# Early convolutions, gate sums and substitution steps of a delta-net and FFN kernel, placed elsewhere

## The chip, the core and the metric

The kernel runs on one core of one Trainium2 chip. The metric is the device time of one execution in microseconds. The core's engines each work through a queue of their own, in the order in which the program issues to them: PE multiplies matrices (PEld is its weight load), DVE, ACT and POOL work on tensors element by element, and SP issues the DMAs. An engine waits where an operand isn't ready or where the place for its result is still being read.

## What is computed

The reference, cut to the parts that the change touches, is a gated delta rule over 4 sequences of 1024 positions with 256 features, followed by a small FFN; each of the two is layer-normed and added to its input:

```python
mixed = einsum('bsh,ch->bsc', x, W_qkv)               # 16 q, 16 k, 32 v heads of 128
conv  = sum(xp[:, i:i+S, :] * conv_w[:, i] for i in range(4))
q, k, v = split(silu(conv))                           # q and k are then normed
beta  = sigmoid(x W_b);  g = -exp(A_log) * softplus(x W_a + dt_bias)
gc    = cumsum(g) within chunks of 64
A     = -(k_beta k^T * exp(gc_i - gc_j)) below the diagonal
Tm    = (I - A)^-1                                    # substitution
u, kcd = Tm v_beta, Tm (k_beta * exp(gc))
# scan over the chunks, with a state St of 128 x 128 for each head and sequence
v_new = u - kcd St
out_i = (q * exp(gc)) St + (q k^T * decay) v_new
St    = St * exp(g_last) + (k * exp(g_last - gc))^T v_new
out   = (rms_norm(out_i) * norm_w * silu(x W_z)) W_out
```

## The kernel before

**Before the main loop** (lines 194 to 281). The rows are read in four blocks of eight tiles, layer-normed and transposed into `xnT`, and the 64 gate columns of every position are summed into `ba` (L225). Then the gates are worked out on tiles of 128 x 1024 (L229 to L257). The cumulative sums follow for eight groups of four heads, one group at a time (L259 to L281): four products with triangular or constant matrices, exponentials on ACT into a table `dk`, a transpose for the rows `prow`, and three stores to DRAM, `rows_d` twice and `dk_d` once. The table `dk` has two buffers.

**The main loop** works on 32 blocks ("supers"), which are 8 groups of heads times 4 stretches of the sequence. Each has 8 units, and a unit is one turn of the loop: s counts from 0 to 255, with 21 early turns ahead of it (s = -21 to -1). A turn works at several stages of the pipeline at once. What it issues to PE, DVE, ACT and POOL is in an order written out by hand: eight strings in `SLOTS`, one for each turn of a round (`iq`, 0 to 7; I call it turn 0 to turn 7; for s >= 0, unit 0 falls on turn 5). SP's queue isn't in this order; it is placed by the framework. The letters are:

- A: one tile of v, and B: one tile of q or k, in the generator `channel`. PE makes the product `pp` in a pair of PSUM banks, ACT writes the first tap of the convolution into `cv` (L437), DVE adds three taps (L440), ACT applies the silu (L444). In the early turns before s = -4 there is only B.
- N0, N1, N2, O3, J, O4: the scan of a unit, in `step`. N0 transposes v (`pv`) and scales it into `x0`. N1 multiplies by the state (`pkqs`, L684), and DVE completes `x0` (L695) while ACT writes `qs` (L696). N2 makes `px` (L704), `xs`, `yg` (L712) and `kt`, and POOL decays the state (L721). In the next turn O3 makes `po` and `core` (L728), J the squares of it on ACT (L733), and O4 `pu` (L741), in a pair of banks, with the state's addition on DVE right behind it (L748).
- Z, T, U: the output projection of an older unit. Z makes `pz` (L143) and its silu; POOL multiplies `zs` twice (L784, L786); T transposes it; U makes `pout` (L797), and DVE adds it into `ac` (L802).
- s and n: scores and norms of a half super. POOL works on `dc` (L530, L531, L537), PE makes `kkq`, DVE `lT` and `aT` (L556), and `n` ends in four small operations on DVE (L488 to L502).
- v with a number: so many steps of the substitution, in `invert`. A step is two operations on DVE, L580 and L581, on (j+1)(31-j) elements for j from 0 to 30, all of it in SBUF. The first call only sets up the tiles.
- b: builds the rest of the inverse from it (`lb`'s copy on ACT, L593; `m1`, `m2` on PE). r and q: small operations of `rms` and the roots.

Two rules order what a letter issues. `go` takes a generator's next part, counts one place on, and then takes up whatever is due; a part that ends with `yield n` is due n places later. A `v` counts no place. `pp` (of A and of B) and `pu` share two pairs of PSUM banks in turn: A, `pu`, B, A, and so on.

A look-up table of the FFN's weights is expanded on POOL in 224 pieces, each a compare (L301) and, but for the first of 16, an addition (L305). One piece is issued behind O4 in every turn, from s = -21 on. From turn 240 the FFN's weights are fetched.

Of the kernel before, what the change touches and what calls it, by code (L numbers as in the profile page):

```python
# [9 lines left out]
F32 = mybir.dt.float32  # L10
I32 = mybir.dt.int32
AF = mybir.ActivationFunctionType
ALU = mybir.AluOpType
# [46 lines left out]
def bc(ap, shape):  # L60
    return ap.to_broadcast(shape)
# [3 lines left out]
def delta_net_ffn_kernel(  # L65
# [128 lines left out]
    with tc.tile_pool(name="pre", bufs=2) as pre, tc.tile_pool(name="gates", bufs=1) as gp:  # L194
# [6 lines left out]
        ba = gp.tile([P, NTILE, 2 * NV], F32, name="ba")  # L201
# [6 lines left out]
        for s in range(NSB):  # L208
# [16 lines left out]
            A.copy(ba[:, s * SB : (s + 1) * SB, :], pg.rearrange("p (t n) -> p t n", n=64))  # L225
        full = [P, NTILE, NV]
        gl = gp.tile(full, F32, name="gl")
        beta = gp.tile(full, F32, name="beta")
        A.activation(beta, ba[:, :, 0:NV], AF.Sigmoid)  # L229
        A.activation(nea, nea, AF.Exp)  # L230
        V.tensor_scalar_mul(nea, nea, -1.0)
        y = gp.tile(full, F32, name="y")
        u = gp.tile(full, F32, name="u")
        w = gp.tile(full, F32, name="w")
        d = gp.tile(full, F32, name="d")
        l = gp.tile(full, F32, name="l")
        V.tensor_tensor(y, ba[:, :, NV:], bc(dtr.unsqueeze(1), full), ALU.add)
# [17 lines left out]
        V.tensor_scalar_max(y, y, 0.0)  # L255
        V.tensor_add(y, y, l)
        V.tensor_tensor(gl, y, bc(nea.unsqueeze(1), full), ALU.mult)  # L257
        nth = NTILE * HG
        for g in range(NG):  # L259
            hs = slice(g * HG, (g + 1) * HG)  # L260
            dk = pre.tile([P, DK], F32, tag="dk", name="dk")
            ps = bank("pgate")
            for i, lhs in enumerate((triu, slow)):
                T_.matmul(ps[:, i * nth : (i + 1) * nth], lhsT=lhs, rhs=gl[:, :, hs], start=True, stop=True)
            A.activation(dk[:, 0 : 2 * nth], ps[:, 0 : 2 * nth], AF.Exp)
            V.tensor_copy(dk[:, 2 * nth : 3 * nth], ps[:, 0:nth])
            ps = bank("pgate")
            for ab in range(2):
                T_.matmul(
                    ps[:, ab * nth : (ab + 1) * nth], lhsT=sel[ab], rhs=gl[:, :, hs], start=True, stop=True  # L270
                )
            el = dk[:, 4 * nth : 6 * nth].rearrange("p (t a h) -> p a t h", a=2, h=HG)
            A.activation(el, ps[:, 0 : 2 * nth].rearrange("p (a t h) -> p a t h", a=2, h=HG), AF.Exp)
            V.tensor_copy(dk[:, 3 * nth : 4 * nth].rearrange("p (t h) -> p t h", h=HG), beta[:, :, hs])
            ps = bank("prow")
            T_.transpose(ps[:, :P], dk[:, 2 * nth : 3 * nth], ident)
            rows = pre.tile([P, P], F32, tag="rows", name="rows")
            A.copy(rows, ps[:, :P])
            for ab in range(2):
                nc.sync.dma_start(rows_d[g, ab], rows[:, ab * C : (ab + 1) * C])  # L280
            nc.sync.dma_start(dk_d[g], dk)  # L281
# [27 lines left out]
    with ExitStack() as main:  # L309
# [80 lines left out]
        def channel(k, blk, n, far):  # L390
# [47 lines left out]
            yield far  # L438
            for i in reversed(range(H)):
                V.scalar_tensor_tensor(cv, ps[:, :, i : i + BT], cw[:, ch, i : i + 1], cv, ALU.mult, ALU.add)  # L440
                if i == H - 1:
                    yield 1
# [215 lines left out]
        def step(k, u):  # L658
# [76 lines left out]
            if not last:  # L735
                pu = two_banks("pu")
                for m in range(MG):
                    two = slice(2 * m, 2 * m + 2)
                    for ab in range(2):
# [3 lines left out]
                        )  # L743
                state = S_.rearrange("p a h d -> p (a h d)")
# [98 lines left out]
        def work(kind, n, *args):  # L843
# [12 lines left out]

        LQ = 2 * SB + 5
        LV = SB // 2
        SLOTS = [
            "A v1 O3 s N0 v1 T n J O4 v1 N1 Z v1 B n N2 U n s",  # L860
            "A v1 O3 N0 v1 T J v1 O4 N1 r Z v1 B N2 q s U",
# [161 lines left out]
        with tc.manual_schedule(engines=COMPUTE):  # L1023
            for s in range(-LQ, len(units)):
# [13 lines left out]
                if nq < len(supers):  # L1038
                    gens["B"] = channel(supers[nq], iq // 4, iq % 4, 1)
# [119 lines left out]
```

## Time and profile before

| | us |
|---|---|
| median of 3 runs (4345.69 to 4350.42) | 4349.83 |
| the profiled execution | 4347.06 |
| its span, first to last instruction | 4345.3 |
| PE / DVE / ACT / POOL busy | 3992.3 / 3517.0 / 2646.9 / 2082.5 |
| before the first tile of the main loop (`pp` starts) | 110.45 |
| mean granted TensorE clock | 0.98 of full |

How it is read: times are in us unless marked ns. A line such as "L440 DVE ... cv<-pp,cw,cv 128x512 ... x1536 | 1148.9, 748 | 352.2 <-ACT cv L437 322.7" gives a line of the kernel, an engine, what is written from what, and the count; then the busy time, the mean length of one in ns, and the engine's idle time just before them with what ended most of it. A line of the timeline gives the start and the length, then the same names, and in brackets the idle time before. In the view by windows a line gives a stretch and its length, then busy time and count of PE, PEld, DVE, ACT and POOL, then the granted clock, the share of the DMA engines and GB/s. A wait for several semaphores is put down to the one that came last by the profile.

### The profile page before, as it was taken

What the parts mean: (1) busy time and instruction counts of PE and PEld (TensorE: products, weight loads), DVE (VectorE), ACT (ScalarE), POOL (GpSimd) and SP (SyncE); (2) the same over time, 40 slices, a digit from 0 to 9 for tenths busy, and PEclk for the clock granted to TensorE, in tenths of its full rate; (3) what the DMA queues carried; (4) which work ended last, traced back from release to release, by engine and by line L of the source; (5) the groups of instructions that cost most, each with busy time, mean ns of one, the idle gap of its engine ahead of it and who ended that gap; (6) DMA issues with size and microseconds to landing.
All of it is one profiled execution on the core that took longest, in us unless ns stands there. A gap on an engine that the chain in (4) does not pass through costs nothing.

```text
span 4345.3 us, 79442 instructions
## 1 busy us (share of the span) xinstructions
PE 3992.3 (92%) x26664; PEld 2858.5 (66%) x26664; DVE 3517.0 (81%) x6641; ACT 2646.9 (61%) x6573; POOL 2082.5 (48%) x1782
## 2 busy tenths in 40 slices
PE   3679999999999999999999999999999999999999
PEld 3456667677666666676766667676766776666454
DVE  4788888888888888888888988888888898886243
ACT  2456667666666666666666666666666666656211
POOL 2545564655555554655455554555554343434122
PEclk7899999999999999999999999999999999999999
DMA  3444444444444454444454444544445444443011
GB/s 88 124 107 113 111 112 124 121 130 119 126 130 118 107 133 125 134 117 119 125 135 128 109 114 128 133 118 114 132 128 128 115 120 121 130 108 96 26 39 29
DMA packets 1053124, 492.72 MB, mean 113 GB/s; under 512 B 730528, under 2 KB 951856, under 8 KB 1052720
## 3 DMA queue, kind: packets, MB, share of 16 engines
q1 hardware_dynamic: 1052720, 487.64, 42.5%
q8 instruction: 216, 3.54, 0.3%
q14 instruction: 188, 1.54, 0.1%
HBM read 267.66 MB, written 219.69 MB: 112 GB/s over the span
## 4 chain that ended last, share of the span: by engine, by line
PE 57%; DVE 25%; issue 7%; ACT 6%; POOL 3%; DMA 1%; SPq 1%; DVEq 0%; POOLq 0%; ACTq 0%
PE pp L423 13%; DVE cv L440 9%; PE pout L797 7%; PE pz L143 7%; PE pkqs L684 6%; DVE rank L580 4%; PE pgu L960 4%; PE px L704 4%; PE pu L741 3%; PE po L704 3%; DVE v L581 2%; PE kkq L546 2%; PE py L976 2%; DVE core L728 2%; PE pto L790 1%
## 5 line engine op out<-in xcount | busy, mean ns | idle before, releaser
L440 DVE SCALAR_TENSOR_TENSOR cv<-pp,cw,cv 128x512 f32<-128x512 f32 x1536 | 1148.9, 748 | 352.2 <-ACT cv L437 322.7
L784 POOL TENSOR_TENSOR zs<-zs,rr 128x512 f32<-128x512 f32 x256 | 267.0, 1043 | 1558.3 <-ACT zs L782 1549.3
L437 ACT ACTIVATE cv<-pp,cw 128x512 f32<-128x512 f32 x512 | 350.9, 685 | 486.0 <-PE pp L423 486.0
L581 DVE TENSOR_TENSOR v<-v,rank 128x31 f32<-128x31 f32 (+15 forms) x992 | 553.3, 558 | 34.1
L423 PE MATMUL pp<-xnT,wq 128*128 128x262 f32 x2048 | 531.0, 401 | 43.3 <-DVE cv L440 34.6
L423 PEld LDWEIGHTS pp<-xnT,wq 128*128 128x128 f32 x2048 | 371.7, 191 | 216.6 <-issue 58.7
L423 PE MATMUL pp<-xnT,wv 128*128 128x262 f32 x2048 | 503.0, 387 | 5.8 <-DVE cv L440 5.8
L797 PE MATMUL pout<-wo,oT 128*128 128x256 f32 x2048 | 504.9, 391 | 0.7 <-ACT oT L792 0.7
L143 PE MATMUL pz<-wzs,xnT 128*64 128x512 f32 x2048 | 487.1, 596 | 4.7 <-DVE ac L802 3.8
L580 DVE TENSOR_TENSOR rank<-v,lb 128x31 f32<-128x31 f32 (+15 forms) x992 | 467.2, 471 | 25.9 <-DMA lb<-ltd 20.1
L684 PE MATMUL pkqs<-S,qku 128*64 128x256 f32 x3840 | 478.1, 387 | 5.2 <-DVE core L728 3.5
L721 POOL TENSOR_TENSOR S<-S,dkm 128x1024 f32<-128x1024 f32 x224 | 436.7, 1949 | 26.5 <-PE pkqs L684 16.1
L704 PE MATMUL px<-x,ue 128*128 128x128 f32 x2048 | 292.9, 287 | 168.2 <-issue 108.1
L704 PEld LDWEIGHTS px<-x,ue 128*128 128x128 f32 x2048 | 264.1, 194 | 269.0 <-issue 151.1
L423 PEld LDWEIGHTS pp<-xnT,wv 128*128 128x128 f32 x2048 | 381.5, 190 | 73.8 <-issue 13.1
L797 PEld LDWEIGHTS pout<-wo,oT 128*128 128x128 f32 x2048 | 384.1, 198 | 49.4 <-issue 3.4
L684 PEld LDWEIGHTS pkqs<-S,qku 128*64 128x64 f32 x3840 | 248.7, 136 | 204.2 <-issue 49.2
L733 ACT ACTIVATE junk<-core 128x128 f32<-128x128 f32 x1024 | 318.5, 311 | 82.4 <-DVE core L728 53.9
L786 POOL TENSOR_TENSOR zs<-zs,core 128x512 f32<-128x512 f32 x256 | 328.6, 1284 | 20.0
L709 ACT ACTIVATE xs<-px 128x512 f32<-128x512 f32 x256 | 154.8, 605 | 236.2 <-PE px L704 236.2
L444 ACT ACTIVATE qk<-cv 128x512 f32<-128x512 f32 x256 | 161.2, 630 | 206.1 <-DVE cv L440 202.6
L741 PE MATMUL pu<-yg,kt 64*128 64x256 f32 x1920 | 272.2, 402 | 14.5 <-DVE cv L440 13.1
(187 smaller groups left out, 7198.4 us busy)
## 6 DMA issues: line engine op xcount, KB each, us to landing
qkd<-qk SPq DMA_DIRECT2D x256, 256.0 KB, 2.6
qku<-qkd SPq DMA_DIRECT2D x256, 256.0 KB, 2.9
dc<-rows_d SPq DMA_DIRECT2D x256, 128.0 KB, 3.4
ltd<-lT SPq DMA_DIRECT2D x128, 256.0 KB, 2.5
atd<-aT SPq DMA_DIRECT2D x128, 256.0 KB, 2.8
ae<-atd SPq DMA_DIRECT2D x512, 64.0 KB, 2.6
acc_d<-ac SPq DMA_DIRECT2D x256, 128.0 KB, 2.2
ac<-acc_d SPq DMA_DIRECT2D x224, 128.0 KB, 2.6
```

The costliest lines, as they stand in the source:

```text
L143: T_.matmul(ps[ab * C : (ab + 1) * C, :], lhsT=xnT[:, kc, 2 * p + ab, H + n * C : H + (n + 1) * C], rhs=rhs(kc), start=kc == 0, stop=kc == ...
L423: T_.matmul(ps[:, 2 * p : 2 * p + 2, : H + BT], lhsT=wt[:, kc, :], rhs=xnT[:, kc, 2 * p : 2 * p + 2, c0 : c0 + H + BT], start=kc == 0, sto ...
L437: A.activation(cv, ps[:, :, H : H + BT], AF.Copy, scale=cw[:, ch, H : H + 1])
L440: V.scalar_tensor_tensor(cv, ps[:, :, i : i + BT], cw[:, ch, i : i + 1], cv, ALU.mult, ALU.add)
L580: V.tensor_tensor(t, bc(v[:, 0 : j + 1, j : j + 1], sh), bc(lb[:, j : j + 1, j + 1 :], sh), ALU.mult)
L581: V.tensor_tensor(v[:, 0 : j + 1, j + 1 :], v[:, 0 : j + 1, j + 1 :], t, ALU.subtract)
L684: T_.matmul(as4(ps)[ab * C : (ab + 1) * C, two, :], lhsT=qk[:, m, j, ab, :], rhs=S_[:, ab, two, :], start=True, stop=True,)
L704: T_.matmul(as4(ps)[:, h, :], lhsT=w[:, h, :], rhs=src[:, h, :], start=True, stop=True)
L721: G_.tensor_tensor(flat, flat, bc(decay, [P, 2 * HG, P]), ALU.mult)
L741: T_.matmul(as4(pu[:, ab])[:, two, :], lhsT=kt[half, m, :], rhs=yg[half, two, :], start=True, stop=True)
L786: G_.tensor_tensor(zs, zs, k.cores.pop(u), ALU.mult)
L797: T_.matmul(pp[:, :HID], lhsT=oT[:, h, :], rhs=wo[:, h, :], start=h == 0, stop=h == HG - 1)
```

## The change

**Gates.** `ba` is laid out by groups of heads when it is copied out of PSUM. The maximum and the addition on `y` become one operation. The table `dk` holds all eight groups, `beta` is copied into it once, and the sums are made for four groups at a time: products with 512 columns instead of 128. The rows come from four products with the gates as the stationary operand, instead of a transpose. The number of stores is the same.

**Early tiles.** For B in the turns s = -20, -18, ..., -6, whose `far` is now 0, the three taps are scaled copies on ACT and additions on POOL, issued at once; for all other tiles the order is as before.

**The turns.** The state's addition behind `pu` is due two places later, which is behind N1. The steps of the substitution stand between A and Z in every turn, and none behind Z. The pieces of the look-up table are issued only from s = 0 on, and by turn: 1, 0, 1, 4, 1, 0, 1, 0.

```diff
@@ gates
-        ba = gp.tile([P, NTILE, 2 * NV], F32, name="ba")
+        ba = gp.tile([P, 2 * NG, NTILE, HG], F32, name="ba")
...
-        V.tensor_scalar_max(y, y, 0.0)
-        V.tensor_add(y, y, l)
-        V.tensor_tensor(gl, y, bc(nea.unsqueeze(1), full), ALU.mult)
...
+        V.scalar_tensor_tensor(l, y, 0.0, l, ALU.max, ALU.add)
+        V.tensor_tensor(by_group(l), by_group(l), heads(nea), ALU.mult)
+        dk = gp.tile([P, NG, DK], F32, name="dk")
+        V.tensor_copy(dk[:, :, 3 * GW : 4 * GW], beta.rearrange("p (g x) -> p g x", g=NG))
+        for gs in range(0, NG, 4):
+            cols = l[:, gs * GW : (gs + 4) * GW]
+            to = dk[:, gs : gs + 4]
             for i, lhs in enumerate((triu, slow)):
...
+                ps = bank("pgate")
+                T_.matmul(ps, lhsT=lhs, rhs=cols, start=True, stop=True)
+                ps = ps.rearrange("p (g x) -> p g x", g=4)
+                A.activation(to[:, :, i * GW : (i + 1) * GW], ps, AF.Exp)
+                if i == 0:
+                    V.tensor_copy(to[:, :, 2 * GW : 3 * GW], ps)
             for ab in range(2):
+                ps = bank("pgate")
+                T_.matmul(ps, lhsT=sel[ab], rhs=cols, start=True, stop=True)
+                el = to[:, :, 4 * GW :].rearrange("p g (t a h) -> p a g t h", a=2, h=HG)[:, ab]
+                A.activation(el, ps.rearrange("p (g t h) -> p g t h", g=4, h=HG), AF.Exp)
+            ps = bank("prow")
+            for i in range(4):
                 T_.matmul(
+                    ps[:, i * P : (i + 1) * P], lhsT=cols[:, i * GW : (i + 1) * GW], rhs=triu, start=True, stop=True
                 )
+            rows = pre.tile([P, 4, P], F32, tag="rows", name="rows")
+            A.copy(rows, ps.rearrange("p (g i) -> p g i", g=4))
+            for i in range(4):
+                for ab in range(2):
+                    nc.sync.dma_start(rows_d[gs + i, ab], rows[:, i, ab * C : (ab + 1) * C])
+                nc.sync.dma_start(dk_d[gs + i], to[:, i])
@@ channel
+            if far:
+                yield far
...
+            else:
+                for i in reversed(range(H)):
+                    t = w1.tile([P, 512], F32, tag="vt", name="tap", bufs=2 * HG).rearrange("p (b t) -> p b t", b=B)
+                    A.activation(t, ps[:, :, i : i + BT], AF.Copy, scale=cw[:, ch, i : i + 1])
+                    G_.tensor_add(cv, cv, t)
@@ step, behind the products pu
+                yield 2
                 state = S_.rearrange("p a h d -> p (a h d)")
@@ the order of the turns
+        PIECES = 1, 0, 1, 4, 1, 0, 1, 0
...
-            "A v1 O3 s N0 v1 T n J O4 v1 N1 Z v1 B n N2 U n s",
-            "A v1 O3 N0 v1 T J v1 O4 N1 r Z v1 B N2 q s U",
-            "A v1 O3 N0 v1 T J v1 O4 v1 N1 Z s v1 B N2 n U",
+            "A v1 O3 s v1 N0 v1 T n J O4 N1 v2 Z B n N2 U n s",
+            "A O3 N0 T J O4 N1 v2 r Z B N2 q s U",
+            "A v1 O3 v1 N0 v2 T J O4 N1 v2 Z s B N2 n U",
             "b A O3 N0 T J O4 N1 Z s B N2 U b",
-            "v1 A b O3 s N0 v1 T n J O4 v1 N1 Z v1 B n N2 v1 U n s",
-            "A v1 O3 N0 v1 T J v1 O4 v1 N1 r Z v1 B N2 q s v1 U",
-            "A v1 O3 N0 v1 T J v1 O4 v1 N1 Z s v1 B N2 n v1 U",
-            "A v1 O3 N0 v1 T J v1 O4 v1 N1 Z s v1 B N2 v1 U",
+            "v1 A b O3 s v1 N0 v1 T n J O4 N1 v2 Z B n N2 U n s",
+            "A O3 N0 T J O4 N1 v2 r Z B N2 q s U",
+            "A v1 O3 v1 N0 v1 T J O4 N1 v2 Z s B N2 n U",
+            "A v1 O3 v1 N0 v2 T J O4 N1 v2 Z s B N2 U",
...
-                    gens["B"] = channel(supers[nq], iq // 4, iq % 4, 1)
+                    gens["B"] = channel(supers[nq], iq // 4, iq % 4, 0 if s < -LV and iq % 2 else 1)
...
-                        next(pieces, None)
+                        for _ in range(PIECES[iq] if s >= 0 else 0):
+                            next(pieces, None)
```

## The prediction

> **What bounds the kernel now.** First the page's busy times, then the windows view by stage, then the waits of PE, then one round of eight turns in the timeline. The busy times and the stage from 290 to 4020 us:
>
> ```profile
> PE 3992.3 (92%) x26664; PEld 2858.5 (66%) x26664; DVE 3517.0 (81%) x6641; ACT 2646.9 (61%) x6573; POOL 2082.5 (48%) x1782
> ```
> ```profile
> 290.00:4020.00 3730.00, 3526.31 (x24655) 2582.50 (x24654) 3220.08 (x5987) 2469.51 (x6242) 1892.63 (x1558) 0.99 0.46 121
> ```
>
> Here the first pair after the stretch is PE. It is busy 3526 of 3730 us, so only 204 us can be won there at most; DVE is busy 86%. The groups by line say where PE stands idle: before `px`, 168 us, put down to "issue"; before `pu`, 14.5 us.
>
> ```profile
> L704 PE MATMUL px<-x,ue 128*128 128x128 f32 x2048 | 292.9, 287 | 168.2 <-issue 108.1
> ...
> L741 PE MATMUL pu<-yg,kt 64*128 64x256 f32 x1920 | 272.2, 402 | 14.5 <-DVE cv L440 13.1
> ```
>
> In the round that I took (`px` of turn 7 at 1005.63 to the next one at 1126.57, 120.95 us) the stalls lie in turns 5, 6 and 7: 2.63, 2.07 and 1.44 us. DVE before the first, and POOL beside it:
>
> ```profile
> 1086.78 2.31 DVE L440 SCALAR_TENSOR_TENSOR cv<-pp,cw,cv 128x512 f32<-128x512 f32 x3
> ...
> 1090.08 0.34 DVE L581 TENSOR_TENSOR v<-v,rank 128x175 f32<-128x175 f32 x1
> 1090.34 1.22 DVE L748 TENSOR_TENSOR S<-pu,S 128x1024 f32<-128x1024 f32 x1
> 1091.47 1.13 DVE L580 TENSOR_TENSOR rank<-v,lb 128x192 f32<-128x192 f32 x1
> 1092.63 1.31 DVE L581 TENSOR_TENSOR v<-v,rank 128x192 f32<-128x192 f32 x1
> 1093.87 1.11 DVE L695 SCALAR_TENSOR_TENSOR x<-pkqs,dkm,x 128x128 f32<-128x128 f32 x4
> ```
> ```profile
> 1091.35 1.04 POOL L784 TENSOR_TENSOR zs<-zs,rr 128x512 f32<-128x512 f32 x1 [2.70 <-ACT zs L782]
> 1092.47 1.26 POOL L786 TENSOR_TENSOR zs<-zs,core 128x512 f32<-128x512 f32 x1
> 1093.69 2.01 POOL L721 TENSOR_TENSOR S<-S,dkm 128x1024 f32<-128x1024 f32 x1
> ```
> ```profile
> 1094.31 1.22 PE L704 MATMUL px<-x,ue 128*128 128x128 f32 x8 [2.63 <-issue]
> ```
>
> The reader is to see three things. `px` waits for `x` (L695), not for "issue": it starts as the first of the four is done. `x` comes late because `S` and a substitution step stand before it on DVE. And **the step is held**: its operations take 1.13 and 1.31 us against 0.34 at 1090.08, each ending 0.2 to 0.3 us after the POOL operation running when it started. Operations with an operand in PSUM (`x` at 1093.87, during L721) are not held. Over a round L580 and L581 take 31 x (0.471 + 0.558) = 31.9 us by their means; unheld, the 31 sizes take some 22 (0.34 twice for the middling, 0.42 twice for the largest): 10 us held. Four small operations of two turns (L754, L755, L502, L496: 0.63, 0.81, 0.75, 0.37 against 0.17) add 4: some 14 in all.
>
> **Part 1, gates.** Time until the product that makes the gates (80.52 + 1.22) is unchanged: of the two operations on `y` the maximum (0.69) had run beside ACT, and the addition (1.23) is replaced by one of its length. Behind it stand, before, eight groups whose table is double buffered, each waiting some 2.4 us for its own store; the first `wq` load is issued at 106.54 as the last store lands. After, per four groups: four products of 512 columns, two passes each at 0.60 (`pgu`, L960) or twice that at half clock, so 4.8 to 9.6 us, and four of 128 columns, 1.2 to 2.4; ACT's five operations of 512 (0.6 each) follow. Two sets: about 14.5 us from 81.9, to 96.5. Then eight row stores at 0.41 and four table stores at 0.38 on SP, 4.8 us: `wq` at about 102. **-4 us**, bounds -10 and 0.
>
> **Part 2, early tiles.** Eight tiles lose three DVE operations (2.32 us) and gain three scaled copies on ACT (0.6 each when pipelined, L437) and three adds on POOL. The add is nowhere in this form; the nearest rows are 1.04 (L784) and 1.28 (L531); I take 1.2. From 115 to 166 us the chain goes ACT `cv` 0.6, DVE 2.36, ACT silu 0.63, then the next tile's `cv`, with nothing beside it: 3.6 us a tile. With the adds, 0.6 + 0.6 + 3.6 + 0.63 = 5.4 to 5.6 us: +1.9 for each of six tiles, +11. The last two tiles lie where DVE is the bound (172 to 222 us): -4.6 for the operations moved, -2.5 for look-up pieces that no longer hold the steps, +3 for adds that hold them: -4. **+6 us**, bounds -5 and +14.
>
> A rule of the Trainium skill weighs on this part. "GPSIMD Engine Reference", section Performance versus the Vector engine, measures an addition of two tensors at 1.96 times VectorE's time; with `yg`'s 0.683 (L712) that is an estimated 1.34 us, and the six tiles would cost +14 rather than +11. No run here shows that add yet.
>
> **Part 3, the turns.** No operation is added per round: 31 steps as before, now 5, 2, 5, 6, 5, 2, 6 in turns 4 to 7 and 0 to 2, and one drained behind turn 2. Moved: `S` goes behind `x`; the step between them goes away; two steps stand behind `S`, ahead of Z; those behind N2 are gone. The four pieces of turn 3 take 4 x 2.4 us on POOL, from 3.9 to 13.5, and `zs`, due near 12 and read 8 us later, can give that: nothing. The pieces begin 21 turns later and end in turn 224 of 256, ahead of the fetch at 240: nothing. SP issues the same DMAs; the drained step delays `lb`'s copy (L593, 2.0) on ACT only when DVE is late.
>
> What goes: the three stalls, 6.1 us a round. What is late next I laid out queue by queue, zero being the `px` of the turn before. From the round: core from 5.7 (`po`'s end), `pu` at 6.5, the first half of `pkqs` done at 8.5, `px` at 14.0. On DVE A's convolution takes 2.2, `x` 1.0, `S` 1.13, `lT` and `aT` 1.2, `yg` 0.6, a step 0.43 to 0.91 by its size. POOL's three (L784, L786, L721; 1.04, 1.26, 1.95, back to back) begin 2.3 us after A's convolution ends (1089.09 to 1091.35, 1105.51 to 1107.85), since ACT's silu, `qs` and `zs` follow it.
>
> That last row decides. Behind the convolution DVE now does its steps, `x` (1.0) and `S` (1.13), so the two moved steps start 2.1 us after it, plus 0.9 for each step in between: **just as POOL's three start**. Turn 5, with no step in between and a convolution ended at 9.0, gets through: steps done at 12.7, no stall. Turn 6: ACT hands A over at 8.55, as now; the convolution, with one step in it that meets a piece (L305), ends at 12.1; step 12.9; `x` 13.9, in time; `S` 15.05. POOL's three run 14.45 to 18.75. The four operations are held by L784, L786 and L721 and end at 19.5, not 16.8. `lT`, `aT`, `yg` and B's convolution end at 23.4, which is 9.4 in turn 7. `pu` takes over B's pair of banks (two pairs are shared by A, `pu` and B) and wanted it at 6.5: PE stalls 2.9. Turn 7: `ac` ends at 9.75, a step 10.6, core 11.2, A's convolution with a step in it 14.2, two steps 16.0, `x` 17.0, `S` 18.1; two of the four operations held, 22.1; B done 26.05, which is 9.1 in turn 0. Turn 0 starts POOL late, since two squares and `junk` stand ahead of `qs` there: one operation held. Turn 1 finds `n`'s small operations held by `dc` (core at 8.2) and its steps by all three. In turn 2 `dc` (L537) and a piece hold the first two steps, and in turn 3 `lb`'s copy comes at 9.7 and A is handed over at 12.4. So:
>
> ```
> turn  A done  x done  S done  POOL's three  steps done  B done (next turn)  PE stall there
>  5     9.0    10.1    11.3    12.4-16.7      12.7           4.3                  0
>  6    12.1    13.9    15.05   14.45-18.75    19.5           9.4                  2.9
>  7    14.2    17.0    18.1    16.55-20.85    22.1           9.1                  2.6
>  0    13.05   15.8    16.9    18.2-22.5      19.6           5.0                  0
>  1    11.0    12.0    13.15   13.35-17.65    18.0           7.9                  1.4 (and 1.0 at B's pp)
>  2    14.4    16.65   17.8    16.75-21.05    21.6           9.0                  2.5
> ```
>
> Turns 4 to 7 and 0 to 3 take 16.5, 13.65, 14.0, 16.95, 16.75, 13.55, 16.5, 16.45: 124.3 against 120.95, **+3.4 us a round**. Holds are 15.7 us between turns 6 and 3 in this table. Each us of hold there is worth 1 us a round, 32 us in all; the round breaks even at 12.3 and reaches PE's own 114.8 at about 6. For the rounds that start a state (one in four, with a stall only in turn 7) I have no other rows and take the same. 32 x 3.4 = **+109 us**; with the holds between 8 and 18, -140 to +180.
>
> **Sum.** The profiled execution took 4347.06 (span 4345.3, 1.8 around it): 4347 - 4 + 6 + 109 = 4458. It stands 2.8 below the median of the runs, 4349.83; I say 4460.
>
> **Rivals.**
> *DVE keeps up, faster.* If the moved steps slip in before POOL's three, or are held less than the one step was at 1091.47, the three stalls go and nothing comes. Decides: holds under 12.3 us a round between turns 6 and 3. For it: no DVE work is added, and turns 5 to 7, where DVE is late now, lose five steps. Against: the 2.3 us row. Price: about 116 us a round, 5 x 32 = 160 less: 4190. Partial cases lie between that and 4340. Chance 0.42.
> *The stall only changes its name.* The 6.1 us come back at `pu`, waiting for L440: 4345 to 4355. Against: an exact balance is a narrow case. Chance 0.05.
> *Deeper.* After a stall of 2.63 us at 972.72 the windows view shows a granted clock of 0.50 for the next 3.4 us. Stalls of 2.5 to 2.9 come three times a round instead of once; one in four catching it (17 such windows stand against some 70 stalls now) adds 20 to 40 us: 4500. Chance 0.12. The Trainium skill, "TensorE: Matmul & The Clock Gate", section What's actually happening, lets the clock fall only after an idle window of about 3.4 us; by that these stalls would cost nothing more, and the row speaks against it.
> *The forecast*, 4380 to 4480: 0.41.
>
> A measurement of this kernel can tell some 0.2% from no change. Slower by more: 0.41 + 0.12 = 0.53; within: 0.05; faster: 0.42. The range takes in the bounds of the holds and most of the faster case, and leaves out about a tenth on either side: 4205 to 4530. The likeliest case's own range is 4380 to 4530.
>
> **What would show it.** Right: the idle time before `px` (168 us) falls below 40, that before `pu` rises from 14.5 to over 150, released by DVE `cv` L440, mostly in turns 7, 0 and 3; L580 and L581 keep means near 471 and 558 ns. Wrong: the means fall to 0.40 us or so and `pu` never waits; then the moved steps did find POOL idle, and the step of this working that fails is "just as POOL's three start". The gates are right if the first `wq` load is issued near 102 us, the early tiles if the odd ones take about 5.5 us from `cv` to silu.

## The result and the profile after

The changed kernel took 4444.27 us (median of 4 runs, 4437.47 to 4450.91), the kernel before 4347.76 beside it (4 runs, 4343.96 to 4350.42): a ratio of **1.0223, 95% interval 1.0200 to 1.0245**. It is slower, as forecast; 4460 was said. The time lies 96.5 us above before. Below, one of ten runs of the kernel with the gates alone (4659 us) and one of five of that with the early tiles alone (12116 us) are left out as slow.

The lines below answer to those of the prediction. First the page's busy times of the changed kernel, then its main loop in the view by windows, in a stretch that is 100 us longer than the one shown of before:

```profile
PE 4035.0 (91%) x26624; PEld 2863.1 (64%) x26624; DVE 3642.8 (82%) x6603; ACT 2655.0 (60%) x6583; POOL 2112.6 (47%) x1806
```
```profile
290.00:4120.00 3830.00, 3567.17 (x24706) 2592.02 (x24704) 3377.22 (x6013) 2468.93 (x6247) 1946.53 (x1602) 0.99 0.45 118
```

DVE is busy for 126 us more with 38 instructions fewer; PE's busy time, too, grew by 43 us for nearly the same products. The groups by line say where PE now stands idle, and which DVE operations grew (the last figure but the releasers is the idle time ahead of the group). First two lines of before that the prediction doesn't show, then the changed kernel:

```profile
L671 PE MATMUL pv<-ident,vt 128*128 128x128 f32 x1024 | 153.6, 273 | 0.0
L790 PE MATMUL pto<-ident,zs 128*128 128x128 f32 x1024 | 154.7, 274 | 14.6 <-DVE yg L712 7.1 <-POOL zs L786 4.3 <-ACT xnT L951 3.2
```
```profile
L757 PE MATMUL pu<-yg,kt 64*128 64x256 f32 x1920 | 288.6, 421 | 67.1 <-DVE cv L450 66.8
L720 PE MATMUL px<-x,ue 128*128 128x128 f32 x2048 | 280.9, 280 | 13.3 <-DVE x L711 4.6 <-issue 3.1 <-ACT junk L749 2.3
L687 PE MATMUL pv<-ident,vt 128*128 128x128 f32 x1024 | 158.2, 277 | 52.0 <-DVE aT L572 42.3 <-DVE yg L728 9.8
L808 PE MATMUL pto<-ident,zs 128*128 128x128 f32 x1024 | 156.9, 276 | 62.6 <-DVE yg L728 53.1 <-POOL zs L804 4.6 <-ACT xnT L971 3.2
```
```profile
L597 DVE TENSOR_TENSOR v<-v,rank 128x31 f32<-128x31 f32 (+15 forms) x992 | 600.5, 605 | 34.1
L596 DVE TENSOR_TENSOR rank<-v,lb 128x31 f32<-128x31 f32 (+15 forms) x992 | 539.3, 544 | 82.7 <-DMA lb<-ltd 70.2
```

Of the 168 us ahead of `px` 155 are gone. In their place PE waits at three places, for DVE's convolution of B (66.8 us) or for `aT` and `yg`, which stand just ahead of it (52.1 and 53.1): 172 us in all. The two operations of a step took 471 and 558 ns before; they take 544 and 605.

How that comes about shows in the same place of a round as in the prediction: `px` of turn 6 and the stretch behind it. DVE:

```profile
1023.63 1.21 DVE L766 TENSOR_TENSOR S<-pu,S 128x1024 f32<-128x1024 f32 x1
1024.76 0.77 DVE L596 TENSOR_TENSOR rank<-v,lb 128x220 f32<-128x220 f32 x1
1025.56 1.34 DVE L597 TENSOR_TENSOR v<-v,rank 128x220 f32<-128x220 f32 x1
1026.93 1.98 DVE L596 TENSOR_TENSOR rank<-v,lb 128x231 f32<-128x231 f32 x1
1028.94 0.40 DVE L597 TENSOR_TENSOR v<-v,rank 128x231 f32<-128x231 f32 x1
1029.26 0.69 DVE L572 TENSOR_TENSOR lT<-kkq,dc 128x512 f32<-128x512 f32 x1
...
1031.71 1.53 DVE L450 SCALAR_TENSOR_TENSOR cv<-pp,cw,cv 128x512 f32<-128x512 f32 x2
```

POOL beside it, then PE:

```profile
1024.24 1.04 POOL L802 TENSOR_TENSOR zs<-zs,rr 128x512 f32<-128x512 f32 x1 [4.47 <-ACT zs L800]
1025.36 1.29 POOL L804 TENSOR_TENSOR zs<-zs,core 128x512 f32<-128x512 f32 x1
1026.62 2.04 POOL L737 TENSOR_TENSOR S<-S,dkm 128x1024 f32<-128x1024 f32 x1
```
```profile
1030.60 0.66 PE L687 MATMUL pv<-ident,vt 128*128 128x128 f32 x4 [0.33 <-DVE aT L572]
1031.94 0.63 PE L808 MATMUL pto<-ident,zs 128*128 128x128 f32 x4 [0.69 <-DVE yg L728]
1033.30 1.13 PE L757 MATMUL pu<-yg,kt 64*128 64x256 f32 x8 [0.73 <-DVE cv L450]
```

Behind the state's addition stand two steps, four operations. POOL starts its three 0.5 us ahead of them. The first operation ends 0.25 us after L802, the second 0.25 us after L804, the third 0.25 us after L737; only the fourth has its own 0.40 us. Unheld the four take 1.6 us; here they take 4.6. B's convolution ends at 1033.2, and PE, which comes upon what hangs on DVE one product after the other, waits a little at each of three.

To count this over a whole trace I took for each of the 1984 step operations the POOL operation that was running at its start, and the time beyond an unheld length of its size. With the median of each size where POOL is idle, over all kernels here, as that length: before, 347 us held in all, 181 of them by POOL's three; after, 467, of them 358 by POOL's three. The expectations below take the lower quartile in the kernel before instead. For one size, 128x135, that is a held length itself (1.03 us; 0.30 with POOL idle), so their totals are 39 us lower in every kernel, while the shares of POOL's three that they name stay within 3 us.

### The profile page after: what moved, and what is told of

The parts are those of the page before. It is cut to its first block, busy times and chain, and to the rows that moved or that the text cites. A ratio compares the mean times of both kernels' runs of the same rounds, so it can differ in the third digit from the quotient of the medians.

```text
span 4448.3 us, 79207 instructions
## 1 busy us (share of the span) xinstructions
PE 4035.0 (91%) x26624; PEld 2863.1 (64%) x26624; DVE 3642.8 (82%) x6603; ACT 2655.0 (60%) x6583; POOL 2112.6 (47%) x1806
## 4 chain that ended last, share of the span: by engine, by line
DVE 41%; PE 35%; ACT 9%; issue 5%; DMA 5%; SPq 2%; POOL 2%; DVEq 0%; ACTq 0%; POOLq 0%
DVE cv L450 10%; PE pp L432 8%; DVE rank L596 8%; DVE v L597 7%; PE pz L143 4%; PE pgu L980 4%; PE pkqs L700 4%; DVE x L711 3%; DVE S L766 3%; PE pout L815 3%; PE px L720 2%; PE pu L757 2%; PE py L996 2%; PE po L720 2%; ACT L550 2%
## 5 line engine op out<-in xcount | busy, mean ns | idle before, releaser
L450 DVE SCALAR_TENSOR_TENSOR cv<-pp,cw,cv 128x512 f32<-128x512 f32 x1512 | 1124.8, 744 | 313.6 <-ACT cv L446 286.1
L802 POOL TENSOR_TENSOR zs<-zs,rr 128x512 f32<-128x512 f32 x256 | 270.3, 1056 | 1613.0 <-ACT zs L800 1613.0
L597 DVE TENSOR_TENSOR v<-v,rank 128x31 f32<-128x31 f32 (+15 forms) x992 | 600.5, 605 | 34.1
L596 DVE TENSOR_TENSOR rank<-v,lb 128x31 f32<-128x31 f32 (+15 forms) x992 | 539.3, 544 | 82.7 <-DMA lb<-ltd 70.2
L700 PE MATMUL pkqs<-S,qku 128*64 128x256 f32 x3840 | 498.2, 400 | 22.8 <-DVE core L744 22.7
L815 PE MATMUL pout<-wo,oT 128*128 128x256 f32 x2048 | 486.2, 380 | 1.2 <-ACT oT L810 0.7
L737 POOL TENSOR_TENSOR S<-S,dkm 128x1024 f32<-128x1024 f32 x224 | 435.1, 1942 | 32.0 <-PE pkqs L700 32.0
L432 PEld LDWEIGHTS pp<-xnT,wv 128*128 128x128 f32 x2048 | 379.7, 189 | 73.0 <-issue 11.4
L700 PEld LDWEIGHTS pkqs<-S,qku 128*64 128x64 f32 x3840 | 259.7, 141 | 235.1 <-DVE core L744 54.2
L815 PEld LDWEIGHTS pout<-wo,oT 128*128 128x128 f32 x2048 | 369.6, 190 | 45.4 <-issue 3.4
L757 PE MATMUL pu<-yg,kt 64*128 64x256 f32 x1920 | 288.6, 421 | 67.1 <-DVE cv L450 66.8
L804 POOL TENSOR_TENSOR zs<-zs,core 128x512 f32<-128x512 f32 x256 | 328.2, 1282 | 20.1
L720 PE MATMUL px<-x,ue 128*128 128x128 f32 x2048 | 280.9, 280 | 13.3 <-DVE x L711 4.6
L143 PEld LDWEIGHTS pz<-wzs,xnT 128*64 128x64 f32 x2048 | 143.1, 138 | 225.2 <-issue 153.1
```

Source lines behind the costliest of these rows:

```text
L143: T_.matmul(ps[ab * C : (ab + 1) * C, :], lhsT=xnT[:, kc, 2 * p + ab, H + n * C : H + (n + 1) * C], rhs=rhs(kc), start=kc == 0, stop=kc == ...
L432: T_.matmul(ps[:, 2 * p : 2 * p + 2, : H + BT], lhsT=wt[:, kc, :], rhs=xnT[:, kc, 2 * p : 2 * p + 2, c0 : c0 + H + BT], start=kc == 0, sto ...
L596: V.tensor_tensor(t, bc(v[:, 0 : j + 1, j : j + 1], sh), bc(lb[:, j : j + 1, j + 1 :], sh), ALU.mult)
L597: V.tensor_tensor(v[:, 0 : j + 1, j + 1 :], v[:, 0 : j + 1, j + 1 :], t, ALU.subtract)
L700: T_.matmul(as4(ps)[ab * C : (ab + 1) * C, two, :], lhsT=qk[:, m, j, ab, :], rhs=S_[:, ab, two, :], start=True, stop=True,)
L720: T_.matmul(as4(ps)[:, h, :], lhsT=w[:, h, :], rhs=src[:, h, :], start=True, stop=True)
```

## The experiments

**The three parts by themselves.** The gates:

```diff
-        ba = gp.tile([P, NTILE, 2 * NV], F32, name="ba")
+        ba = gp.tile([P, 2 * NG, NTILE, HG], F32, name="ba")
...
+        for gs in range(0, NG, 4):
```

Expected:

> Only the gates are changed. By the traces the first tile of the main loop starts 8.7 us earlier after the change (101.71 against 110.45): if the gates alone do that and the loop behind them runs on unchanged, 8 to 10 us less than before. The prediction's step had 4 less. Rival: the main loop takes up what the start gives (its first loads come no earlier), then 0 to 2 less.

Measured: 4342.51, ratio 0.9986 (0.9977 to 0.9996), 6 us less. The first `pp` comes 4.8 us earlier than before and the first `px` 5.5. In this trace `ba` is complete at the same time as before (55.37 and 55.38). In that of the changed kernel it was complete at 52.17, and over the seven traces whose gates are as before it is complete between 48.99 and 55.82. So 3.2 of the 8.7 us that the expectation goes by lie ahead of what the gates' change touches, and are scatter between runs.

The early tiles:

```diff
-                    gens["B"] = channel(supers[nq], iq // 4, iq % 4, 1)
+                    gens["B"] = channel(supers[nq], iq // 4, iq % 4, 0 if s < -LV and iq % 2 else 1)
```

Expected:

> Only the eight early tiles are changed; the look-up pieces and the steps stay where they were. By the traces the stretch from the first tile to the first px grew from 147.25 to 171.1 us, 23.8 more. If the tiles on ACT and POOL make that: 18 to 28 us slower than before, and more if the look-up pieces, which are still on POOL here, stand in front of the additions (each 2.4 us). The prediction's step: 6 slower. Rival, that the growth comes from the steps and pieces moved in the early turns: 0 to 8 slower here, and it shows in the kernel with the turns alone.

Measured: 4368.86, ratio 1.0044 (1.0027 to 1.0061), 21 us more. From the first `pp` to the first `px` it takes 171.7 us, 24.5 more than before. The tiles make it, not the pieces or steps.

The turns (order of the steps, pieces, and the later addition):

```diff
+                yield 2
                 state = S_.rearrange("p a h d -> p (a h d)")
...
-            "A v1 O3 N0 v1 T J v1 O4 v1 N1 Z s v1 B N2 v1 U",
+            "A v1 O3 v1 N0 v2 T J O4 N1 v2 Z s B N2 U",
```

Expected:

> Only the turns are changed: the state's addition two places later, the steps between A and Z, the pieces by turn. The first px to the last took 89.5 us more after the change. If that is of the turns alone: 80 to 95 us slower than before, less a few us for early turns without pieces. The prediction's step: 109 slower. Rival, that the early tiles or the gates shift something the whole loop then carries: under 50 slower.

Measured: 4420.68, ratio 1.0161 (1.0142 to 1.0181), 72 us more. From the first `px` to the last it takes 84 us more (3853.7 against 3769.3). The first `px` comes 7.5 us earlier, but the pieces missing from the early turns don't show as the reason: `ba` was complete 6.1 us earlier in this trace, and from the first `pp` to the first `px` it is 1.0 us less. The three parts, -6, +21 and +72, make 87 of the 96.5; each of the four medians has a spread of some us, so they add up as far as can be told.

**The turns taken apart.** The later addition alone:

```diff
+                yield 2
                 state = S_.rearrange("p a h d -> p (a h d)")
```

Expected:

> Only the state's addition is made two places later; steps and pieces stand as before. Theory: what makes the change slow is that steps stand behind the state's addition, where POOL's three hold them; the later addition by itself is good, since x no longer waits for it. Then the stalls at px (168 us) mostly go, the steps keep means near 471 and 558 ns, and the time falls by 60 to 160 us. Rival: the later addition gives the pair of banks of pu back later and pushes POOL's decay and DVE's next work, so the stalls come back at pu or pp and the time stays within 20 us of before, or gets slower.

Measured: **4287.27, ratio 0.9858 (0.9843 to 0.9873), 61 us less.** The group lines of this kernel:

```profile
L704 PE MATMUL px<-x,ue 128*128 128x128 f32 x2048 | 286.5, 283 | 17.1 <-DVE x L695 9.6 <-ACT qs L696 2.1 <-ACT junk L733 1.1
L741 PE MATMUL pu<-yg,kt 64*128 64x256 f32 x1920 | 272.2, 402 | 71.5 <-DVE cv L440 71.0 <-DVE rank L580 0.4
```

Of the 168 us at `px` 151 are gone, and 57 of them come back at `pu`. The rival saw the place, but not the sum. The steps are held 269 us here, 109 by POOL's three: less than before, since fewer steps now meet the two multiplications of `zs`.

The other half, the order of steps and pieces without the later addition:

```diff
-            "A v1 O3 N0 v1 T J v1 O4 v1 N1 Z s v1 B N2 v1 U",
+            "A v1 O3 v1 N0 v2 T J O4 N1 v2 Z s B N2 U",
```

Expected:

> The kernel before with the change's order of the steps and its pieces, but the state's addition where it was, behind pu. The addition now stands ahead of x, and the two steps behind x start when they do in the changed kernel. With all of the turns' change the kernel took 4420, with the addition alone 4287. Theory (the place of the steps costs, whatever the addition does): holds by POOL's three stay over 250 us, and x is late by the addition besides: 4400 to 4480. Rival (only the two together do harm, since the addition ahead of the steps pushes them onto POOL's three): 4300 to 4350.

Measured: 4412.22, ratio 1.0142 (1.0127 to 1.0158), 64 us more; POOL's three hold the steps for 346 us. With the kernel before at 4348 the two halves make a table (the lower right is the kernel with the turns alone; the right column has the change's pieces too):

```
                         steps as before   steps between A and Z
addition behind pu            4348                 4412
addition two places later     4287                 4421
```

The place of the steps costs with either. The gain of the later addition is lost in the lower right: PE then waits for B's convolution, no longer for `x`.

**Is it the holds, or only the order?** The changed kernel, with POOL's three as multiplications by a constant:

```diff
-            G_.tensor_tensor(zs, zs, bc(k.rr[u // 4][:, u % 4, :].unsqueeze(2), h4), ALU.mult)
+            G_.tensor_scalar_mul(zs, zs, 0.5)
...
-            G_.tensor_tensor(zs, zs, k.cores.pop(u), ALU.mult)
+            k.cores.pop(u)
+            G_.tensor_scalar_mul(zs, zs, 0.5)
...
-                    G_.tensor_tensor(flat, flat, bc(decay, [P, 2 * HG, P]), ALU.mult)
+                    G_.tensor_scalar_mul(flat, flat, 0.5)
```

Expected:

> The changed kernel, but POOL's three are multiplications by a constant (one tensor in place of two); left out are the gates on zs, the product of zs with core, and the state's own decay factors. Of the 992 steps the trace of the changed kernel has 385 held by POOL's three, 356 us above their unheld lengths, while the 296 steps that started during a look-up compare, which has one tensor as operand, are 3 to 11 us longer all together in the two traces. Theory (the two steps behind the state's addition are held by POOL's three, and that makes DVE late): the holds by the three fall from 356 to under 40 us though POOL works no less, PE's stalls fall from 275 to under 110 us, the half-clock windows fall too, and the time falls by 110 to 200 us from 4444, to 4245 to 4335: ahead of the kernel before. Rival (the order alone: steps stand ahead of B's convolution, five or six in one turn, and DVE would be late without holds): the time stays within 50 us of 4444.

Measured: **4197.36, ratio to before 0.9656 (0.9642 to 0.9671)**: 247 us below the changed kernel, more than the theory's range. The groups of POOL and of the steps in this kernel:

```profile
L737 POOL TENSOR_SCALAR S<-S 128x1024 f32<-128x1024 f32 x224 | 626.8, 2798 | 28.6 <-PE pkqs L700 28.6
L805 POOL TENSOR_SCALAR zs<-zs 128x512 f32<-128x512 f32 x256 | 390.1, 1524 | 21.3
L802 POOL TENSOR_SCALAR zs<-zs 128x512 f32<-128x512 f32 x256 | 386.9, 1512 | 1140.0 <-ACT zs L800 1139.8
```
```profile
L597 DVE TENSOR_TENSOR v<-v,rank 128x31 f32<-128x31 f32 (+15 forms) x992 | 416.8, 420 | 34.1
L596 DVE TENSOR_TENSOR rank<-v,lb 128x31 f32<-128x31 f32 (+15 forms) x992 | 365.6, 369 | 91.5 <-DMA lb<-ltd 70.1 <-POOL v L589 5.7 <-POOL lt L310 3.2
```

POOL's three take longer than before, 5.8 us a turn in place of 4.3, and hold much less: 53 us in place of 358. DVE has the same 6603 instructions, and its busy time falls from 3642.8 to 3171.0 us. The same stretch as above, DVE and then POOL:

```profile
977.39 0.38 DVE L596 TENSOR_TENSOR rank<-v,lb 128x220 f32<-128x220 f32 x1
977.80 0.39 DVE L597 TENSOR_TENSOR v<-v,rank 128x220 f32<-128x220 f32 x1
978.22 0.40 DVE L596 TENSOR_TENSOR rank<-v,lb 128x231 f32<-128x231 f32 x1
978.66 0.69 DVE L597 TENSOR_TENSOR v<-v,rank 128x231 f32<-128x231 f32 x1
```
```profile
976.88 1.50 POOL L802 TENSOR_SCALAR zs<-zs 128x512 f32<-128x512 f32 x1 [4.63 <-ACT zs L800]
978.46 1.51 POOL L805 TENSOR_SCALAR zs<-zs 128x512 f32<-128x512 f32 x1
```

The four operations are done 2.0 us after the first began (977.39 to 979.35), with POOL busy throughout. Three have their own length. The fourth, which begins 0.20 us into L805, takes 0.69 us where it took 0.40 in the changed kernel: these operations on POOL hold a step too, but only one that begins soon after them (the last section has the count). PE's idle time between the first and the last `px` falls from 269 (the expectation has 275) to 86 us. (`zs` no longer needs `core` and `rr` here; in the changed kernel POOL's group lines show no wait for either.) The rival, order alone, falls: the order is the same, and the time is 247 us less.

The same three multiplications in the kernel before, as its base line:

Expected:

> The kernel before, with the same three multiplications by a constant; left out are the gates on zs, the product with core and the state's decay factors. It is the base line for the kernel above: in the kernel before POOL's three hold 225 steps by 182 us. Theory: the stalls at px (168 us) fall to under 60, the time falls by 70 to 130 us, less than the changed kernel gains by the same. Rival (the holds are not what makes x late; it is late because the state's addition stands ahead of it): stalls at px stay over 120 us and the time falls by under 40.

Measured: 4232.75, ratio 0.9737 (0.9722 to 0.9751), 115 us less; idle time at `px` 54 us. So with most of these holds gone the change is a gain: from the first `px` to the last it then takes 3605.8 us, the kernel before with the same multiplications 3648.3. The sign of the whole change hangs on the holds.

**Where to put the steps instead.** The changed kernel with the two steps ahead of N1:

```diff
-            "A v1 O3 v1 N0 v2 T J O4 N1 v2 Z s B N2 U",
+            "A v1 O3 v1 N0 v2 T J O4 v2 N1 Z s B N2 U",
```

Expected:

> The changed kernel, with the two steps behind N1 put ahead of it: in seven strings 'O4 N1 v2' becomes 'O4 v2 N1'. The steps of each turn stay as many, 5, 2, 5, 6, 5, 2, 6 in turns 4 to 7 and 0 to 2; they now follow A's convolution at once, some 2.3 us ahead of POOL's three, and x and the state's addition follow them. Theory (the place behind the state's addition is what costs): the holds by POOL's three fall from 356 to under 120 us, the stalls from 275 to under 160, and the time falls by 100 to 180 from 4444, to 4264 to 4344. Rival (too many steps in one turn, wherever they stand): x is late by 1.7 us, the stalls come back at px, and the time stays over 4400.

Measured: 4283.08, ratio 0.9844 (0.9830 to 0.9857): **161 us below the changed kernel**, for the two steps moved past N1 in seven of the strings. At the same `px` the last operation of a step begins 0.26 us ahead of POOL's three, and keeps its own length:

```profile
995.05 0.40 DVE L597 TENSOR_TENSOR v<-v,rank 128x231 f32<-128x231 f32 x1
```
```profile
995.31 1.04 POOL L802 TENSOR_TENSOR zs<-zs,rr 128x512 f32<-128x512 f32 x1 [4.66 <-ACT zs L800]
```

POOL's three hold 69 us of steps in this kernel, and `pu` waits 0.8 us in all. The rival has a part: `x` comes later, `px` waits 104 us, 64 of them in turn 7, which has six steps.

**The burst of pieces.** One piece a turn:

```diff
-        PIECES = 1, 0, 1, 4, 1, 0, 1, 0
+        PIECES = 1, 1, 1, 1, 1, 1, 1, 1
```

Expected:

> The changed kernel with one look-up piece in every turn from s = 0, in place of 1, 0, 1, 4, 1, 0, 1, 0. Turn 3 is the turn that grew most (13.73 to 17.19 us in the mean, 111 us in all), and POOL works on four pieces there. Theory (the turns after the held steps wait, and turn 3 because turn 2's steps are held): the four pieces are worth little, the time stays within 25 us of 4444, and turn 3 stays over 16.5 us. Rival (the four pieces hold zs back, or hold DVE's steps, in turn 3): turn 3 falls under 15 us and the time by 60 us or more.

Measured: 4455.29, ratio 1.0244 (1.0227 to 1.0261), 11 us above the changed kernel. Turn 3 takes 17.08 us, as with the burst (17.19): not the burst makes it long. Spread out, the pieces' additions hold the steps for 41 us instead of 27.

**Early tiles: the wait on ACT.** The early tiles alone, with the silu of an odd tile two places later:

```diff
-            yield 2
+            yield 2 if far else 4
             A.activation(dst, cv.rearrange("p (q a) (n t) -> p n q a t", a=2, n=2), AF.Silu)
```

Expected:

> The kernel with the early tiles alone (4370, 22 above before), with the silu of an odd early tile issued two places later, as that of the other tiles is. It changes ACT's order in three turns only: there the exponentials of the scores and two loads of a function table stand ahead of the silu that waits for POOL's additions, no longer behind it. In the trace of the early tiles the silu waits 2.9 to 5.2 us for POOL, and the exponentials, in the kernel before hidden beside DVE's convolution, come after it. Theory (half of the loss is work that queued behind this wait): 6 to 13 us less, 4357 to 4364. Rival (the longer chain of one tile is all of it): within 3 us of 4370.

Measured: 4362.00, ratio 1.0030 (1.0020 to 1.0039), 7 us below 4368.86. ACT in an odd tile, first with the early tiles alone, then with the silu later:

```profile
167.91 1.84 ACT L448 ACTIVATE tap<-pp,cw 128x512 f32<-128x512 f32 x3
172.66 0.63 ACT L451 ACTIVATE qk<-cv 128x512 f32<-128x512 f32 x1 [2.91 <-POOL cv L449]
173.31 1.28 ACT L541 ACT_TABLE_LOAD   x1
174.60 1.15 ACT L541 ACTIVATE dc<-dc 128x512 f32<-128x512 f32 x2
```
```profile
164.74 1.84 ACT L448 ACTIVATE tap<-pp,cw 128x512 f32<-128x512 f32 x3
166.59 1.28 ACT L541 ACT_TABLE_LOAD   x1
167.89 1.15 ACT L541 ACTIVATE dc<-dc 128x512 f32<-128x512 f32 x2
169.06 1.28 ACT L451 ACT_TABLE_LOAD   x1
170.35 0.63 ACT L451 ACTIVATE qk<-cv 128x512 f32<-128x512 f32 x1
```

In the upper fence the silu stands 2.91 us in ACT's queue and waits for POOL's additions, and the exponentials, which need nothing of it, wait behind. In the lower one they fill that gap. By the medians it is a third of the loss, not half as I had put it. In the traces the stretch from the first `pp` to the first `px` falls by 4.8 us, from 171.7 to 166.9, a fifth of the 24.5 that the tiles added there.

**A version that beats both.** Gates and later addition, and an order with no step between N1 and N2:

```diff
-            "A v1 O3 N0 v1 T J v1 O4 v1 N1 Z s v1 B N2 n U",
+            "A v1 O3 N0 v1 T v1 J v1 O4 v1 N1 Z s B N2 v1 n U",
...
-            "A v1 O3 N0 v1 T J v1 O4 v1 N1 r Z v1 B N2 q s v1 U",
-            "A v1 O3 N0 v1 T J v1 O4 v1 N1 Z s v1 B N2 n v1 U",
+            "A v1 O3 N0 v1 T J v1 O4 v1 N1 Z B r N2 q s v1 U",
+            "A v1 O3 N0 v1 T J v1 O4 v1 N1 Z s B N2 n v1 U",
```

Expected:

> The kernel before with the gates of the change, the state's addition two places later, and an order of its own: no step between N1 and N2, where POOL's three run; the steps freed there stand in turn 2, ahead of N1 and behind N2, and r stands behind B. Pieces and early tiles as before. The kernel with the later addition alone took 4287, and its steps were held 231 us, 110 of them by POOL's three. Theory: holds by the three fall under 50 us, the stalls at pu (71 us) halve, and the time is 4287 - 5 (gates) - 25 to 60 = 4220 to 4257. Rival (moving steps again only moves the wait; turn 2 with six steps makes px late in turn 2 or b late): 4270 to 4330.

Measured: 4228.62, ratio 0.9726 (0.9712 to 0.9741). `pu` waits 7.4 us in place of 71.5. POOL's three still hold 67 us, not under 50: behind N2 some steps meet them or the multiplication of `dc`.

The same with the change's list of pieces:

```diff
-                        next(pieces, None)
+                        for _ in range(PIECES[iq] if s >= 0 else 0):
+                            next(pieces, None)
```

Expected:

> The order of its own (the kernel that took 4228.6, with the gates and the later addition), and the pieces by the change's list: none in the early turns, then 1, 0, 1, 4, 1, 0, 1, 0, with four in turn 3, where no steps stand. In the kernel with the order alone the look-up additions hold 79 steps by 36 us, and px waits 22 us in turn 1, where a piece and zs run on POOL beside the last steps. Theory (a burst of pieces costs nothing where DVE has no steps, and a turn without a piece frees its steps): holds by the pieces fall under 20 us, the stall in turn 1 under 8, the early turns are 5 to 8 us shorter (in the kernel with the turns alone the first px came 7 earlier); 4200 to 4217. Rival (turn 3's stalls at pz and pu in the changed kernel were of the burst): turn 3 grows from 13.95 to over 14.5 us and the time stays over 4225.

Measured: **4217.31, ratio 0.9700 (0.9686 to 0.9713)**, 3.0% below the kernel before; by the medians it lies 227 us below the changed one. The stall in turn 1 falls from 22 to 4 us, and turn 3 takes 14.03 us: the burst is free where DVE has no steps. The early turns were expected to be shorter and are not: the first `px` comes 5.2 us earlier, but the first `pp` 7.5, and between the two it takes 2.3 us longer (149.1 against 146.8). The pieces still hold 26 us, not under 20, and `pz` waits 26 us in turn 2, where it waited 9.

## Why the prediction was right, and where it was off

**The sum, 4460 against 4444: closer than its terms.** The turns were put at +109 and cost 72 by themselves (84 in the loop), the early tiles at +6 and cost 21. The two misses lie on opposite sides and cancel in part, which is luck. That it gets slower, and at which place, is not: the experiments show the mechanism. But the sign had only 0.53 of the chance.

**The stalls at `px` go: right.** Below 40 was said, 13.3 is left.

**"Just as POOL's three start": right, and shown.** Steps moved out of that place (161 us), POOL's operations changed so that they hold little (247 us), and the two halves of the turns by themselves all say the same.

**The steps "keep means near 471 and 558": wrong.** They rose to 544 and 605. My table let the holds go from 14 us a round, steps and small operations, to 15.7 between turns 6 and 3; the steps alone went from 10.9 to 14.6 (347 and 467 us over 32 rounds). The step that failed is the balance behind those means: I let old holds go as new ones came. What went was 87 us (`dc` held 153 us before and 66 after), what came was twice that (POOL's three, 181 and 358).

**"pu takes over B's pair of banks ... PE stalls": right in kind, mis-sized.** Over 150 us at `pu` were said, 67.1 came. PE takes its products in order, and `pv` and `pto` stand ahead of `pu`; they hang on `aT` and `yg`, which stand ahead of B's convolution on the same late DVE. I had looked only at the last of the three waits; together they are 172 us.

**+3.4 us a round, +109 in all: 89.5 came.** Between the first and last `px` 24848 products had 55.6 us more idle time (213 to 269) and took 33.9 us more themselves (3556 to 3590). The windows at half the granted clock grew from 65 to 97 us in that stretch. At half speed that is at most 16 of the 33.9; the rest stays open. So the rival "Deeper" was no alternative but at most a part of it, under a fifth. Even that is not shown: the kernels with the gates alone and the early tiles alone have 82 and 79 us of such windows with loops at most 7 us longer than before's, and that with the steps alone has 55 with a loop 75 us longer. By rounds, cut at `px` of turn 6 (cut at turn 7, as in the prediction, the three rows are +3.8, +1.1 and +2.5):

```
                                    rounds   forecast each   measured each
full rounds                           21         +3.4            +3.9
rounds that start a state              7         +3.4            +0.3
the last three                         3         +3.4            +0.7
```

The full rounds were sized well. "I have no other rows and take the same" failed: in six rounds of a fresh state turn 7 fell from 17.7 us to 14.1, where it grew in the others. By turns the table hit turns 0, 1, 4, 5 and 6 within 0.15 us (16.75, 13.56, 16.50, 13.54 and 13.87 in the median); turn 2 is 1.8 shorter than forecast, turn 7 0.7 shorter, turn 3 1.1 longer.

**"Reaches PE's own 114.8 at about 6" fits.** In the changed kernel with one-tensor multiplications the steps are held 109 us, 3.4 a round, and the median round takes 115.5 us. In the last kernel above, of another order, they are held 6.7 a round and the round takes 116.4.

**Gates: -4 said, 6 measured for the whole kernel: right.** "Time until the product that makes the gates is unchanged" held: from the end of `ba` to the end of that product it takes 26.36 us in both traces (55.38 to 81.74, and 52.17 to 78.53). From there to the first `wq` load it takes 20.6 us where 24.8 were, and 20.3 were said; to the first `pp` 5.5 us less. The first `wq` was issued at 99.17, not near 102, because all of it began 3.2 us earlier. The terms behind the 20.3 were off both ways: "Two sets: about 14.5 us" took 11.4, to 89.9; "Four table stores ... 4.8 us" was too short, since the 24 stores ran from 84.7 to 96.8 and SP's queue ended last, not PE.

**Early tiles: +6 said, with bounds of -5 and +14; 21 measured.** "+1.9 for each of six tiles" is where it failed. An odd tile with nothing beside it took 5.8 us from `cv` to the next `cv`, 2.2 more: the chain itself was about right, and so was 1.2 for the addition (1.28). But I had not asked what is queued behind the waiting silu: three of the eight odd tiles took up to 5.6 us more, because the exponentials with their table loads no longer lay beside DVE's convolution. The experiment gives 7 us for that by the medians, 4.8 in the traces, and six chains of 2.2 are 13: together most of the 21; the rest stays open. The estimate worked out from the Trainium skill, "GPSIMD Engine Reference", Performance versus the Vector engine, was 1.34 us for the addition; 1.28 was measured.

**The rival "DVE keeps up, faster"** named its condition well: holds under 12.3 us a round. They were above (14.6 a round, by the steps alone); where an experiment on the changed kernel took them to 3.4 or 3.7, it was faster than before. The chance of 0.42 for it was fair for a case that the place of one letter decides.

## What to carry to other kernels

An operation moved to a "free" place on its engine has to be checked against what the other engines do in that place: here a DVE operation on two SBUF tensors that started under a POOL operation on two tensors ended no earlier than that one in 547 of 555 cases, however short it was itself. When a long operation is deferred, look at what slides into its place before you add more there; here the deferral alone was worth 61 us, and the steps put behind it, with the new list of pieces, cost 133. And where an engine is given an operation that waits for another engine, list what is queued behind it, and issue that first.

## What the runs showed of the hardware

A step's operation that began under a POOL TENSOR_TENSOR was held until 0.1 to 0.3 us after it (the medians by line); of 555 in the changed kernel 8 ended before it, which began within 0.03 us of it. With POOL idle, the 1224 operations in the kernel before lost nothing. Under a POOL TENSOR_SCALAR it was held for a part of that operation only. In the changed kernel with such multiplications, 172 of the 441 step operations that began under L802 or L805 lost 0.30 us each. All of them began in the first 0.41 us and ended, in the median, 0.85 to 0.89 us after the start of an operation of 1.5 us; those that began later lost nothing. In its base line 95 of 321 that began under L721 lost 49 us. All began in its first 0.76 us and ended 1.29 us after its start, well inside its 2.77 us. One of them, 0.37 us long with POOL idle, and POOL beside it:

```profile
1071.68 1.25 DVE L581 TENSOR_TENSOR v<-v,rank 128x207 f32<-128x207 f32 x1
```
```profile
1071.67 2.77 POOL L721 TENSOR_SCALAR S<-S 128x1024 f32<-128x1024 f32 x1
```

POOL waits as well, but for less, since a step's operation is short (at most 0.43 us). In the changed kernel L737 takes 1.90 us when the step under which it starts has less than 0.2 us to go, and 2.08 when it has more than 0.3.

The Trainium skill, "SBUF — State Buffer", section SBUF: two separate sides, gives this as an exclusive lock between a DVE operation with two SBUF inputs and any GpSimd operation that reads SBUF, held for the whole instruction, in which the one that comes second waits. The runs agree for two tensors on POOL, on both sides. For one tensor on POOL, which is read from SBUF as well, the hold ends some 0.6 us (of 1.5) and 1.5 us (of 2.77) before the operation does.

The one-tensor form is the slower one on POOL itself: 2.80 us against 1.94 for 128x1024, 1.51 against 1.06 and 1.28 for 128x512.
